# A graph attention kernel: the adjacency turned as packed bytes on VectorE instead of TensorE

## The chip, the core and the metric

The kernel runs on one core of a Trainium2 chip. A core has engines that run side by side, each with its own queue of instructions, taken in order: TensorE (PE in the profile; PEld is its weight load), VectorE (DVE), ScalarE (ACT), GpSimd (POOL), and SyncE (SP), which here only issues DMAs. SBUF is the working memory of 128 partitions, PSUM the memory into which TensorE writes. The metric is the device time of one execution in microseconds; lower is better.

## The reference

Sixty-four graphs of 256 nodes with 512 features go through two layers of attention. `adj` holds one boolean per pair of nodes, and its diagonal may be empty.

```python
def attention(x, mask, heads):                    # both layers, shortened
    q, k, v = heads_of(x @ w_qkv)                 # layer 0: 4 heads of 64; layer 1: 8 heads
    s = einsum('bhid,bhjd->bhij', q, k) * 64 ** -0.5
    s = where(mask[:, None], s, very_negative)
    return (softmax(s) @ v).reshape(...) @ w_out + b_out

h = maximum(layernorm(x), 0);  x = x + attention(h, adj, 4)
h = maximum(layernorm(x), 0);  x = x + attention(layernorm(h) * gamma + beta, adj | eye, 8)
```

A row of layer 0 without any neighbour has equal weights for all keys. Layer 1 always lets a node see itself. All of it is float32.

## The kernel before, in words

**Tiling.** The program takes two graphs at a time (`G = 2`), so there are 32 steps, `s` from 0 to 31. The 512 tokens of a step lie as four blocks of 128 partitions (`NT = 4`). Projections and output products are matrix products by seven block products instead of eight (`PRODUCT`), so each stage is a set of seven groups of matmuls, with sums of blocks made on VectorE and GpSimd (`act_sums0`, `act_sums1`, L404 to L410). Products 4 and 7 of a set share one PSUM bank, as do 2 and 1, and 3 and 5 (`SHARED`): the second of a pair accumulates on top of the first, after the first has been read by `evacuate` (L746) or `accumulate` (L765). Four banks serve these products (`mm_tile`) and four the scores.

**Scores lie transposed:** keys on the partitions, queries along the row. Therefore the mask is needed transposed too. The bytes of `adj` are loaded with query rows on the partitions (`load_adjacency`, L486). Until now `adjacency_cast` (L511) makes them bfloat16 on GpSimd, `adjacency_turn` (L557) turns eight blocks of 128x128 on TensorE into one PSUM bank, and ScalarE copies the bank to `adT` (L568). From `adT`, GpSimd makes the additive masks: `mask0` (L570) for layer 0, which is (value - 1) * 1e30 and then times `ne`, so that a row without neighbours gets zeros; and `mask1` (L579) for layer 1, in which the diagonal is cleared by `offdiag`. `mask_scores` (L988) adds a mask to the scores, `exponentials` (L995) follows on ScalarE. The sums over keys come from `key_halves` (L1000, GpSimd, into `pd`), `turn_keys` (L1007, VectorE's transpose of 32x32 blocks), `key_quarters` (L1013), `turn_sums` (L1064) and `key_sums` (L1074); `normalise` (L1114) multiplies the weighted values by their inverses on GpSimd.

**The order is written out by hand.** `at(period, place, fn, ...)` notes a call with a place in time; at the end all calls are sorted by place and emitted. Each engine takes its instructions in that order. A period is 6.4 places long (6.2 before period 0), and in a full one these stages follow each other on TensorE, each with seven products (`at_set`), the evacuation of product i being placed at its end, at (i + 1) / 7:

- 0.0: the first query and key projection of layer 1 of step s
- 1.0: `combine` of layer 1 of step s - 1, the output product, with the order of products 1, 5, 2, 6, 7, 3, 4
- 2.0 (`AT_X`): a `visit`, which weighs the values of layer 0 of step s + 1 and makes scores of layer 1 of step s; then the value projection `project_v1`, with the order 1, 6, 5, 2, 7, 3, 4
- 3.0: `combine` of layer 0 of step s + 1, whose result is added to `xt`
- 3.5, 4.5, 5.5, 6.2: the second projection of layer 1, a visit, the projections of layer 0 of step s + 2, a visit

So three steps are in work at once. The work on the adjacency of step s + 2 lies in period s: cast at 0.45, turn at 2.5 (in the middle of the value projection), `mask0` at 3.1, `mask1` at 5.85. The bias `bo` of layer 0 is added to `xt` before the output product arrives, by `first_bias` (L506): four instructions on GpSimd, one per block of 128 tokens, at 2.34 and 2.5 for blocks 2 and 3 and at 2.85 and 2.86 for blocks 0 and 1. Steps 0 and 1 have places of their own in a start that is denser (`FIRST_Q0` and its like); there the row `ne` is also turned by TensorE.

Lines that the prediction's steps touch besides: L402 (sums of weights, early in the program), L530 (`neighbours_line`), L606 (`scale_row` on ScalarE), L623 and L600 to L602 (row scales on GpSimd), L675 (`transpose_h` on TensorE), L700 (`turn_blocks`, VectorE's transposes of `h`), L749 to L763 (`evacuate`), L770 to L785 (`accumulate`), L817 and L898 and L914 (matmuls of the projections, the values and the combination), L970 (scores), L1041 (weighing).

Of the kernel before, what the change touches and what calls it, by code (L numbers as in the profile page):

```python
# [8 lines left out]
FP = mybir.dt.float32  # L9
BF = mybir.dt.bfloat16  # L10
U8 = mybir.dt.uint8
I32 = mybir.dt.int32
AF = mybir.ActivationFunctionType
ALU = mybir.AluOpType

EPS = 1e-5
BIG = 1e30
# [298 lines left out]
def fast_path(  # L316
# [19 lines left out]
    nc = tc.nc  # L336
    P = 128
    B, N, D = x.shape
    DH = 64
    G = 2  # L340
    NSTEP = B // G
    NIC = N // P
    NT = G * NIC
# [9 lines left out]
    act = ctx.enter_context(tc.tile_pool(name="act", bufs=1))  # L353
# [10 lines left out]
    def mm_tile(shape, dt=FP, hold=False):  # L364
        tag = next(b for b in banks if b not in held)
        banks.remove(tag)
        banks.append(tag)
        if hold:
            held.add(tag)
        return ps_mm.tile(shape, dt, name="mm", tag=tag)  # L370

    identb = const.tile([P, P], BF, name="identb")
# [17 lines left out]


    NB = 7
    A_OF = {(0, 0): 0, (0, 1): 1, (1, 0): 2, (1, 1): 3}
    B_OF = ((0, 6, 5), (1, 3, 1))
    PRODUCT = {1: (0, 0), 2: (1, 1), 3: (6, 2), 4: (3, 6), 5: (2, 3), 6: (4, 4), 7: (5, 5)}
# [18 lines left out]
    HC, HP0, HP1 = NC // 2, PR0 // 2, PR1 // 2  # L414
    wqk0 = const.tile([P, NB, HC, 2, H0], FP, name="wqk0")
    wv0 = const.tile([P, NB, HC, I0 // 2], FP, name="wv0")
    wo0 = const.tile([P, NB, HP0, HD], FP, name="wo0")
    wqkv1 = const.tile([P, NB, HC, 3, H1], FP, name="wqkv1")
    wo1 = const.tile([P, NB, HP1, HD], FP, name="wo1")
    bo_b = const.tile([P, D], FP, name="bo_b")  # L420
# [42 lines left out]
    def weight_block(wr, n, c):  # L463
# [3 lines left out]
        for i in range(2):  # L467
            blk = A_OF[i, c // HC]
            dst = wqkv1[:, blk, c % HC, n, :] if n < 3 else wo1[:, blk, c % HC, :]
# [4 lines left out]
    S = [dict() for _ in range(NSTEP)]  # L474
# [28 lines left out]
            S[s]["xt"][:, g * NIC:(g + 1) * NIC], x[s * G + g].rearrange("(t p) d -> p t d", p=P)  # L503
        )

    def first_bias(s, t):  # L506
        xt = S[s]["xt"]
        nc.gpsimd.tensor_tensor(xt[:, t, :], xt[:, t, :], bo_b, ALU.add)  # L508


    def adjacency_cast(s):  # L511
        S[s]["adb"] = act.tile([P, NT, N], BF, name="adb", tag="ab")
        nc.gpsimd.tensor_copy(S[s]["adb"], S[s]["ad"])

    def neighbours(s, g):

# [37 lines left out]
        ne = S[s]["ne"] = act.tile([P, T], FP, name="ne")  # L554
        nc.scalar.copy(ne, pn)

    def adjacency_turn(s):  # L557
        adb = S[s]["adb"]
        pa = mm_tile([P, NIC, G, N], BF)
        for g in range(G):  # L560
            for kc in range(NIC):
                for ic in range(NIC):
                    nc.tensor.transpose(  # L563
                        pa[:, kc, g, ic * P:(ic + 1) * P],
                        adb[:, g * NIC + ic, kc * P:(kc + 1) * P], identb,
                    )
        S[s]["adT"] = act.tile([P, NIC, G, N], BF, name="adT", tag="ab")
        nc.scalar.copy(S[s]["adT"], pa)  # L568

    def mask0(s):  # L570

        st = S[s]
        n0 = st["n0"] = act.tile([P, NIC, G, N], BF, name="n0")
        nc.gpsimd.tensor_scalar(n0, st["adT"], -1.0, BIG, op0=ALU.add, op1=ALU.mult)
        for kc in range(NIC):
            v = n0[:, kc].rearrange("p g n -> p (g n)")
            nc.gpsimd.tensor_tensor(v, v, st["ne"], ALU.mult)

    def mask1(s):  # L579
        st = S[s]  # L580
        n1 = st["n1"] = act.tile([P, NIC, G, N], BF, name="n1", bufs=2)
        nc.gpsimd.tensor_scalar(n1, st["adT"], -1.0, BIG, op0=ALU.add, op1=ALU.mult)
        for kc in range(NIC):
            v = n1[:, kc, :, kc * P:(kc + 1) * P]
            nc.gpsimd.tensor_tensor(v, v, offdiag, ALU.mult)
# [82 lines left out]
    def transpose_h(s, lyr, c):  # L668
        st = S[s]
        if c == 0:  # L670
            st["hT"] = act.tile([P, NB, HC, N], FP, name="hT")
        ph = mm_tile([P, G, N])
# [20 lines left out]
    Q, NQ = 32, P // 32  # L693
# [432 lines left out]
    def at(period, place, fn, *args):  # L1126
        events.append((period * (PERIOD if period >= 0 else FIRST) + place, len(events), fn, args))
# [68 lines left out]
    AT_X, AT_C0, AT_QK, AT_Q0, AT_V0, AT_H1, AT_Z = 2.0, 3.0, 3.5, 4.5, 5.5, 6.06, 6.2  # L1196
# [8 lines left out]
    p = NSTEP - 2  # L1205
# [9 lines left out]
    FIRST_C0, FIRST_Q0, FIRST_V0, FIRST_H1 = 3.0, 3.64, 4.64, 5.2  # L1215
# [5 lines left out]
    for s in range(NSTEP):  # L1221

        p = s - 2
        if s == 1:
            p -= 3.93 / FIRST
        at(p - 1 if s != 1 else -2, 3.2 if s == 1 else 5.7 if s < 3 else AT_H1 + 0.01, load_h, s)
        at(p - 1 if s != 1 else -2, 3.2 if s == 1 else 5.7 if s < 3 else 1.0, load_adjacency, s)
        at(p, (2.0, 2.4)[s] if s < 2 else 0.45, adjacency_cast, s)
        for t in range(NT):
            at(p, (0.5 + 0.4 * t, 1.95 + 0.1395 * t)[s] if s < 2 else (0.95, 1.05, 1.2, 1.35)[t], norm0, s, t)  # L1230
            if s == 0:
# [15 lines left out]
        else:  # L1247
            at(p, 2.3 if s == 2 else 0.05, neighbours_line, s)
            at(p, 2.31 if s == 2 else 0.051, neighbours_spread, s)
        at(p, (FIRST_Q0 + 0.1425, 3.583)[s] if s < 2 else 2.5, adjacency_turn, s)  # L1250
        at(p, (FIRST_Q0 + 0.3, 3.74)[s] if s < 2 else 3.1, mask0, s)
        at(p, (FIRST_Q0 + 0.31, 4.43)[s] if s < 2 else 5.85, mask1, s)
        if s == 0:
            at(p, FIRST_C0, first_transposes)
        else:
# [19 lines left out]
        p = s - 1  # L1275
        if s == 0:
            p -= 2.23 / FIRST
        edge = 0 if s == 0 else 1 if s == NSTEP - 1 else 2
# [3 lines left out]
            at(p, AT_X - 0.000145 if s > 1 else 1.2, load_graph, s, 1)  # L1282
            at(p, AT_X + 0.0051 if s > 1 else 1.2, load_graph, s, 0)
        for k, t in enumerate(NORM1):
            at(p, (1.55, 1.5, (2.34, 2.5, 2.85, 2.86)[k])[edge], first_bias, s, t)
        if edge == 2:
            at(p, 2.8, lambda s=s: act_sums0(S[s]["oT0"]))
            at(p, 2.81, lambda s=s: act_sums1(S[s]["oT0"]))
# [26 lines left out]
        p = s  # L1315
        if s < NSTEP - 1:
# [3 lines left out]
            p, place = (s + 1, 1.0) if s < NSTEP - 2 else (s, LAST_QK + 2)  # L1320
# [5 lines left out]
        else:  # L1326
            p = s - 1
# [39 lines left out]
def kernel(tc, *args):  # L1367
    nc = tc.nc
    B, N, _ = args[0].shape
    P = 128  # L1370
    with tc.tile_pool(name="guard", bufs=1) as guard:
        extremes = guard.tile([P, B // 2 * 3 + 4], FP, name="extremes")
        ident = guard.tile([P, P], FP, name="ident")
        make_identity(nc, ident)
        fast_path(tc, *args, ident, extremes)
        safe = guard.tile([1, 1], I32, name="safe")
        with tc.tile_pool(name="gps", bufs=1, space=bass.MemoryType.PSUM) as ps:
            top = guard.tile([P, 1], FP, name="top")
            nc.vector.tensor_reduce(top, extremes, axis=mybir.AxisListType.X, op=ALU.max)
            row = ps.tile([1, P], FP, name="row")  # L1380
            nc.tensor.transpose(row, top, ident)
            all_top = guard.tile([1, 1], FP, name="all_top")
            nc.vector.tensor_reduce(all_top, row, axis=mybir.AxisListType.X, op=ALU.max)
            nc.vector.tensor_scalar(safe, all_top, LIMIT, None, op0=ALU.is_le)
        flag = nc.values_load(safe[0:1, 0:1], min_val=0, max_val=1, skip_runtime_bounds_check_because="a comparison gives 0 or 1")
        with tc.If(flag < 1):
            general_path(tc, *args)
# [29 lines left out]
```

## Time and profile before

| | |
|---|---|
| median of 3 runs | 3113.7 us (3112.78 to 3113.93) |
| profiled execution, its own time | 3115.69 us |
| its span, first to last instruction | 3113.6 us |
| TensorE busy, matmuls | 3091.8 us, 20362 instructions |
| VectorE busy | 2453.8 us, 4371 instructions |
| ScalarE busy | 1235.3 us, 2166 instructions |
| GpSimd busy | 2242.3 us, 2128 instructions |
| L563, TensorE's transposes of the adjacency | 256, 19.5 us busy |
| L568, ScalarE's copy of them | 32, 32.4 us busy |
| L513, GpSimd's cast of the bytes | 32, 33.2 us busy |
| L508, GpSimd's adds of `bo` | 128, of which 124 on `xt`: 156.3 us busy |

How to read it: the span is what the trace covers; the execution's own time has a little around it. Busy time is the union of an engine's instructions. In a timeline, the columns are the start, the duration, the engine, line and operation, what is written from what, shapes, how many neighbouring instructions were merged (x4), and in brackets how long the engine was idle before and what ended that. The granted clock of TensorE was 1.0 throughout.

### The profile page before, as it was taken

The page shows a single profiled execution, that of the slowest core. Times are in us where ns is not written, and L with a number is a line of the kernel's source. Part 1 is how long each engine was busy: PE and PEld are TensorE (multiplying, and loading weights), DVE is VectorE, ACT ScalarE, POOL GpSimd, SP SyncE. Part 2 cuts the span into 40 slices and gives each one's busy share as a digit, 9 for nine tenths or more (in the row PEclk, how much of TensorE's full clock was granted, in tenths as well). Part 3 has the DMA queues.
Part 4 walks back from the last instruction along what each step waited for, and adds up shares of the span by engine and source line. Part 5 has one row for each costly group of instructions (what it writes and reads, how often), then busy time and mean ns, then how long its engine had stood idle before and what let it go on. Part 6 is the DMA issues. An engine that isn't in the chain of part 4 may idle for free.

```text
span 3113.6 us, 55568 instructions
## 1 busy us (share of the span) xinstructions
PE 3091.8 (99%) x20362; PEld 2538.7 (82%) x20362; DVE 2453.8 (79%) x4371; ACT 1235.3 (40%) x2166; POOL 2242.3 (72%) x2128
## 2 busy tenths in 40 slices
PE   8999999999999999999999999999999999999998
PEld 6888888888888888888888888888888888888787
DVE  6877877878877788787788777887777878778766
ACT  4434343344434343443434334443434344343431
POOL 7877776777767767767777677776776776777753
PEclk9999999999999999999999999999999999999999
DMA  4233232332322322223313233222232222331311
GB/s 138 64 98 92 55 91 72 92 93 67 83 71 87 93 87 66 84 72 99 93 53 93 72 91 93 73 79 77 80 93 86 67 82 74 99 93 51 91 34 49
DMA packets 187589, 251.22 MB, mean 81 GB/s; under 512 B 58088, under 2 KB 78192, under 8 KB 187312
## 3 DMA queue, kind: packets, MB, share of 16 engines
q1 hardware_dynamic: 139088, 183.74, 21.0%
q10 hardware_dynamic: 48224, 63.87, 7.0%
q8 instruction: 164, 2.69, 0.4%
q14 instruction: 113, 0.93, 0.1%
HBM read 128.59 MB, written 34.34 MB: 52 GB/s over the span
## 4 chain that ended last, share of the span: by engine, by line
PE 94%; POOL 3%; DMA 1%; DVE 1%; issue 1%; SPq 0%; ACT 0%; ACTq 0%; POOLq 0%; DVEq 0%
PE mm L817 37%; PE mm L914 17%; PE mm L898 11%; PE sc L970 8%; PE mm L864 6%; PE sc L1041 6%; PE mm L1041 5%; PE mm L970 2%; POOL pd L1005 1%; POOL xt L508 1%; PE mm L847 1%; DMA h<-blocks 0%; PE mm L940 0%; DMA out_dram<-xt 0%; PE mm L563 0%
## 5 line engine op out<-in xcount | busy, mean ns | idle before, releaser
L817 PE MATMUL mm<-hT,wqkv 128*128 128x256 f32 x3584 | 788.3, 380 | 0.6 <-DVE qk L757 0.6
L817 PEld LDWEIGHTS mm<-hT,wqkv 128*128 128x128 f32 x3584 | 677.6, 190 | 103.2 <-issue 11.4
L1005 POOL TENSOR_TENSOR pd<-p 128x512 f32<-128x512 f32 x383 | 479.4, 1273 | 337.9 <-ACT p L998 196.2
L914 PE MATMUL mm<-wo,oT 128*128 128x256 f32 x2632 | 586.1, 380 | 4.2 <-DVE xt L774 2.4
L914 PEld LDWEIGHTS mm<-wo,oT 128*128 128x128 f32 x2632 | 497.3, 190 | 83.2 <-issue 9.2
L998 ACT ACTIVATE p<-p 128x512 f32<-128x512 f32 x766 | 440.8, 626 | 118.2 <-DVE p L993 106.2
L993 DVE TENSOR_TENSOR p<-sc,n 128x512 f32<-128x512 f32 x579 | 363.0, 683 | 145.1 <-PE sc L970 145.1
L898 PE MATMUL mm<-wqkv,hT 128*128 128x256 f32 x1792 | 402.1, 382 | 0.4 <-ACT v L751 0.4
L817 PE MATMUL mm<-hT,wqk 128*128 128x256 f32 x1792 | 398.7, 382 | 0.3 <-ACT qk L751 0.2
L817 PEld LDWEIGHTS mm<-hT,wqk 128*128 128x128 f32 x1792 | 338.3, 191 | 55.9 <-issue 10.3
L898 PEld LDWEIGHTS mm<-wqkv,hT 128*128 128x128 f32 x1792 | 335.5, 190 | 54.2 <-issue 10.3
L970 PE MATMUL sc<-qk 64*128 64x256 f32 x2320 | 294.0, 385 | 1.7 <-DVE p L993 1.7
L785 POOL TENSOR_TENSOR xt<-xt,u 128x512 f32<-128x512 f32 x183 | 231.2, 1272 | 78.2 <-DVE xt L774 37.1
L970 PEld LDWEIGHTS sc<-qk 64*128 64x128 f32 x2320 | 218.1, 186 | 62.8 <-issue 27.9
L1011 DVE STREAM_TRANSPOSE turned_p<-pd 128x1024 f32<-128x1024 f32 x192 | 237.1, 1235 | 29.5 <-POOL pd L1005 29.5
L606 ACT ACTIVATE h<-h,mr,r 128x512 f32<-128x512 f32 x252 | 187.6, 803 | 169.6 <-POOL mr L602 169.6
L1116 POOL TENSOR_TENSOR oT<-oT 128x512 f32<-128x512 f32 x188 | 240.0, 1277 | 2.2 <-DMA oT<-line 2.2
L1018 DVE TENSOR_REDUCE part<-turned_p 128x32 f32<-128x1024 f32 x192 | 233.2, 1215 | 4.4
L1041 PE MATMUL sc<-p,v 128*32 128x256 f32 x3152 | 190.8, 382 | 0.0
L864 PE MATMUL mm<-hT,wv 128*128 128x256 f32 x840 | 188.6, 382 | 0.0
L864 PEld LDWEIGHTS mm<-hT,wv 128*128 128x128 f32 x840 | 156.5, 190 | 27.2 <-ACT vT L751 6.2
L1041 PE MATMUL mm<-p,v 128*32 128x256 f32 x2976 | 177.6, 379 | 0.0
(153 smaller groups left out, 4219.2 us busy)
## 6 DMA issues: line engine op xcount, KB each, us to landing
h<-blocks SPq DMA_DIRECT2D x960, 64.0 KB, 2.0
oT<-line SPq DMA_DIRECT2D x376, 128.0 KB, 3.1
h<-in_x_dram SPq DMA_DIRECT2D x31, 1024.0 KB, 8.7
xt<-in_x_dram ACTq DMA_DIRECT2D x60, 512.0 KB, 4.3
out_dram<-xt SPq DMA_DIRECT2D x31, 512.0 KB, 3.1
out_dram<-xt ACTq DMA_DIRECT2D x31, 512.0 KB, 4.5
v<-values ACTq DMA_DIRECT2D x480, 32.0 KB, 1.9
ne<-ne SPq DMA_DIRECT2D x90, 64.0 KB, 2.0
```

The lines of the kernel that those rows point to most:

```text
L817: nc.tensor.matmul(bank[:, k, :], w[:, wa, c, k, a * P:(a + 1) * P], st["hT"][:, ba, c, :], start=first and (k, c) == (0, 0), stop=(k, c) ...
L864: nc.tensor.matmul(bank, wv0[:, wa, c, :], st["hT"][:, ba, c, :], start=first and c == 0, stop=c == HC - 1, skip_group_check=True,)
L898: nc.tensor.matmul(bank[:, t, :], st["hT"][:, ba, c, t * P:(t + 1) * P], wqkv1[:, wa, c, 2, :], start=first and (t, c) == (0, 0), stop=(t, ...
L914: nc.tensor.matmul(bank[:, t, :], oT[:, ba, c, t * P:(t + 1) * P], w[:, wa, c, :], start=first and (t, c) == (0, 0), stop=(t, c) == (NIC - ...
L970: nc.tensor.matmul(sc[g][e][:, kc, :], qk[rows, 1, k0:k0 + P], qk[rows, 0, g * N:(g + 1) * N], start=True, stop=True,)
L993: nc.vector.tensor_tensor(p[e][:, g], sc[e], neg[:, :, g, :], ALU.add)
L998: nc.scalar.activation(p[e][:, g], p[e][:, g], AF.Exp, scale=SCALE)
L1005: nc.gpsimd.tensor_tensor(st["pd"][:, e], p[e][:, :, 0, :], p[e][:, :, 1, :], ALU.add)
L1011: nc.vector.transpose(st["turned_p"], st.pop("pd").rearrange("p e g (b k) -> p (e g b) k", k=32))
L1018: nc.vector.tensor_reduce(st["part", lyr, prs][:, i], st.pop("turned_p"), axis=mybir.AxisListType.X, op=ALU.add)
L1041: nc.tensor.matmul(po[r0:r0 + 32, g, :], (st["v1"][:, g * NIC + kc, pr * P + r0:pr * P + r0 + Q] if lyr else st["v0"][:, r0 // Q, pr, g * ...
L1116: nc.gpsimd.tensor_tensor(dst, dst, invb, ALU.mult)
```

## The change

The bytes are never made bfloat16. Four blocks of 128 query rows lie side by side for the same key, so that one byte from each makes one 32-bit word: GpSimd writes each byte plus 64 (`MARK`) to every fourth place of a tile `both`, which makes each word an ordinary float32 number. VectorE then transposes these words in 32x32 blocks: a call of `adjacency_turn(s, a)` has four instructions, which read partition group `a` and write partition groups 0 to 3; four calls turn everything. The masks read the turned bytes, at every fourth place, and subtract the mark again. TensorE's eight transposes and ScalarE's copy are gone, and with them the use of a PSUM bank.

In full periods three of the calls stand behind the evacuations of the fourth, fifth and sixth product of `combine` of layer 1, and the fourth at the end of that stage behind `turn_blocks`. In steps 0 and 1 the calls stand behind evacuations of the first projections, and `mask0` and `mask1` come later there.

Two of the four pieces of `first_bias` in steps 1 to 30 move from GpSimd (2.34 and 2.5) to VectorE, at 2.6 and 2.61, within the value projection. The other two stay on GpSimd at 2.87 and 2.88.

```diff
-    def first_bias(s, t):
+    def first_bias(s, t, eng=nc.gpsimd):
         xt = S[s]["xt"]
-        nc.gpsimd.tensor_tensor(xt[:, t, :], xt[:, t, :], bo_b, ALU.add)
+        eng.tensor_tensor(xt[:, t, :], xt[:, t, :], bo_b, ALU.add)
-    def adjacency_cast(s):
-        S[s]["adb"] = act.tile([P, NT, N], BF, name="adb", tag="ab")
-        nc.gpsimd.tensor_copy(S[s]["adb"], S[s]["ad"])
+    def adjacency_pack(s):
+        both = S[s]["both"] = act.tile([P, 2, NIC, P, NT], U8, name="both", tag="ab")
+        nc.gpsimd.tensor_scalar(
+            both[:, 0].rearrange("p k j t -> p t k j"), S[s]["ad"].rearrange("p t (k j) -> p t k j", j=P),
+            MARK, None, op0=ALU.add,
+        )
+    def adjacency_turn(s, a):
+        words = S[s]["both"].rearrange("p h k j t -> p (h k j t)").bitcast(FP).rearrange(
+            "p (h k j) -> p h k j", h=2, k=NIC
+        )
+        for b in range(NQ):
+            nc.vector.transpose(
+                words[b * Q:(b + 1) * Q, 1, :, a * Q:(a + 1) * Q], words[a * Q:(a + 1) * Q, 0, :, b * Q:(b + 1) * Q]
+            )
+    def edges(s):
+        return S[s]["both"][:, 1].rearrange("p k i t -> p k t i")
-    def adjacency_turn(s):
...
-                    nc.tensor.transpose(
-                        pa[:, kc, g, ic * P:(ic + 1) * P],
-                        adb[:, g * NIC + ic, kc * P:(kc + 1) * P], identb,
-                    )
-        S[s]["adT"] = act.tile([P, NIC, G, N], BF, name="adT", tag="ab")
-        nc.scalar.copy(S[s]["adT"], pa)
...
-        nc.gpsimd.tensor_scalar(n0, st["adT"], -1.0, BIG, op0=ALU.add, op1=ALU.mult)
+        nc.gpsimd.tensor_scalar(
+            n0.rearrange("p k g (c i) -> p k (g c) i", i=P), edges(s), -1.0 - MARK, BIG, op0=ALU.add, op1=ALU.mult
+        )
...
-        at(p, (FIRST_Q0 + 0.1425, 3.583)[s] if s < 2 else 2.5, adjacency_turn, s)
-        at(p, (FIRST_Q0 + 0.3, 3.74)[s] if s < 2 else 3.1, mask0, s)
-        at(p, (FIRST_Q0 + 0.31, 4.43)[s] if s < 2 else 5.85, mask1, s)
+        for a in range(NQ):
+            at(
+                p, (FIRST_Q0, 3.3)[s] + (a + 3) / 7 - 0.0005 if s < 2 else AT_X - 0.00031 if a > 2 else 1 + (a + 4) / 7 - 0.0005,
+                adjacency_turn, s, a,
+            )
+        at(p, (FIRST_Q0 + 0.87, 4.2)[s] if s < 2 else 3.1, mask0, s)
+        at(p, (FIRST_Q0 + 0.88, 4.43)[s] if s < 2 else 5.85, mask1, s)
...
-            at(p, (1.55, 1.5, (2.34, 2.5, 2.85, 2.86)[k])[edge], first_bias, s, t)
+            if edge < 2 or k > 1:
+                at(p, (1.55, 1.5, 2.85 + 0.01 * k)[edge], first_bias, s, t)
+            else:
+                at(p, 2.6 + 0.01 * k, first_bias, s, t, nc.vector)
```

`mask1` changes in the same way as `mask0`.

More of the change, by code (lines that the diff above doesn't have):

```diff
@@ L392, in fast_path @@
     NB = 7
+    MARK = 64.0
     A_OF = {(0, 0): 0, (0, 1): 1, (1, 0): 2, (1, 1): 3}
@@ L555, in neighbours_turn @@
         nc.scalar.copy(ne, pn)
-    def adjacency_turn(s):
[L558 to L563, printed above, removed]
-                        pa[:, kc, g, ic * P:(ic + 1) * P],
-                        adb[:, g * NIC + ic, kc * P:(kc + 1) * P], identb,
-                    )
-        S[s]["adT"] = act.tile([P, NIC, G, N], BF, name="adT", tag="ab")
-        nc.scalar.copy(S[s]["adT"], pa)
     def mask0(s):
@@ L581, in mask1 @@
         n1 = st["n1"] = act.tile([P, NIC, G, N], BF, name="n1", bufs=2)
-        nc.gpsimd.tensor_scalar(n1, st["adT"], -1.0, BIG, op0=ALU.add, op1=ALU.mult)
+        nc.gpsimd.tensor_scalar(
+            n1.rearrange("p k g (c i) -> p k (g c) i", i=P), edges(s), -1.0 - MARK, BIG, op0=ALU.add, op1=ALU.mult
+        )
         for kc in range(NIC):
@@ L1227, in fast_path @@
         at(p - 1 if s != 1 else -2, 3.2 if s == 1 else 5.7 if s < 3 else 1.0, load_adjacency, s)
-        at(p, (2.0, 2.4)[s] if s < 2 else 0.45, adjacency_cast, s)
+        at(p, (2.0, 2.4)[s] if s < 2 else 0.45, adjacency_pack, s)
         for t in range(NT):
@@ L1249, in fast_path @@
             at(p, 2.31 if s == 2 else 0.051, neighbours_spread, s)
-        at(p, (FIRST_Q0 + 0.1425, 3.583)[s] if s < 2 else 2.5, adjacency_turn, s)
-        at(p, (FIRST_Q0 + 0.3, 3.74)[s] if s < 2 else 3.1, mask0, s)
-        at(p, (FIRST_Q0 + 0.31, 4.43)[s] if s < 2 else 5.85, mask1, s)
+        for a in range(NQ):
+            at(
+                p, (FIRST_Q0, 3.3)[s] + (a + 3) / 7 - 0.0005 if s < 2 else AT_X - 0.00031 if a > 2 else 1 + (a + 4) / 7 - 0.0005,
+                adjacency_turn, s, a,
+            )
+        at(p, (FIRST_Q0 + 0.87, 4.2)[s] if s < 2 else 3.1, mask0, s)
+        at(p, (FIRST_Q0 + 0.88, 4.43)[s] if s < 2 else 5.85, mask1, s)
         if s == 0:
```

## Prediction

> **What bounds it now.** I read busy shares and chain first, then PE's timeline of one step, then VectorE's and GpSimd's beside it. The page:
>
> ```profile
> PE 3091.8 (99%) x20362; PEld 2538.7 (82%) x20362; DVE 2453.8 (79%) x4371; ACT 1235.3 (40%) x2166; POOL 2242.3 (72%) x2128
> PE 94%; POOL 3%; DMA 1%; DVE 1%; issue 1%; SPq 0%; ACT 0%; ACTq 0%; POOLq 0%; DVEq 0%
> ```
>
> TensorE ends the program: 94% of the chain is its own work. The chain in order of time gives the length of a step (first projection of one period to that of the next), and PE's timeline in that step shows the transposes:
>
> ```profile
> 1515.08 12.28 PE mm L817 x56
> 1610.75 12.28 PE mm L817 x56
> ...
> 1546.62 7.17 PE L898 MATMUL mm<-wqkv,hT 128*128 128x256 f32 x32
> 1553.63 0.61 PE L563 MATMUL mm<-identb,adb 128*128 128x128 bf16 x8
> 1554.08 5.40 PE L898 MATMUL mm<-wqkv,hT 128*128 128x256 f32 x24
> ```
>
> A step is 95.67 us and most are exactly that: PE is full, so microseconds taken from or added to its queue count one for one.
>
> **Step 1, transposes leave PE.** The durations of single matmuls overlap (0.22 each), so I take starts: 1554.08 - 1553.63 = 0.45 us per step. Thirty steps: -13.6 us. The first two sets, at 15.8 and 48.2, gain nothing: PE then waits for an evacuation anyway (0.23 for ACT's copy at 16.67, 0.20 for VectorE's L753 at 49.17). The Trainium skill ("VectorE: DVE Perf Modes", The three transpose paths) prices a bf16 128x128 transpose at 390 ns on TensorE and 311 ns on VectorE. By it eight would cost PE 3.1 us and the estimated gain would be 94 us; the trace has 0.45 us for eight in a row, and it decides. ACT loses its 1.01 us copy (L568); at 40% busy that is worth nothing.
>
> **Step 2, 16 transposes of 32 partitions x 64 words enter VectorE.** L1071 has this size: 0.96 us for four in a row, so 3.84 us per step. VectorE in the old place and the new one:
>
> ```profile
> 1534.30 0.69 DVE L772 TENSOR_TENSOR u<-mm,u 128x512 f32<-128x512 f32 x1
> 1536.03 0.69 DVE L774 TENSOR_TENSOR xt<-mm,xt 128x512 f32<-128x512 f32 x1 [1.04 <-PE mm L914]
> 1537.76 0.69 DVE L781 TENSOR_TENSOR xt<-mm,xt 128x512 f32<-128x512 f32 x1 [1.03 <-PE mm L914]
> 1539.48 0.69 DVE L779 TENSOR_TENSOR xt<-mm,xt 128x512 f32<-128x512 f32 x1 [1.03 <-PE mm L914]
> 1540.09 2.48 DVE L700 STREAM_TRANSPOSE blocks<-h 128x512 f32<-128x512 f32 x4
> 1544.13 2.48 DVE L993 TENSOR_TENSOR p<-sc,n 128x512 f32<-128x512 f32 x4 [1.56 <-PE sc L970]
> ...
> 1553.46 0.68 DVE L755 TENSOR_TENSOR v<-mm,v 128x512 f32<-128x512 f32 x1
> 1556.06 0.69 DVE L757 TENSOR_TENSOR v<-mm,v 128x512 f32<-128x512 f32 x1 [1.92 <-PE mm L898]
> ```
>
> The four groups fall into the idle 1.04, 1.03, 1.03 and 1.56: hidden by PE's combine and weighing. Bounds: 0.20 us each (32x32, L1071) to 0.31 (L530, 32x128, 1.23 for four). At 0.31 the first three end 0.2, 0.4 and 0.6 late; behind them wait the evacuations L774, L781, L779, whose banks PE wants again a whole product (1.73) later, and 0.3 of lateness is left at L993, at most 0.3 us of PE. I take 0.24 and nothing. No gain is possible.
>
> **Step 3, the two adds of xt and bo_b on VectorE.** They queue between L755 (ends 1554.14) and L757, into the last gap above. Alone such an add takes 0.69 (L408 on VectorE at the end of the program), two 1.3: they would fit. But both inputs lie in SBUF, while GpSimd is running:
>
> ```profile
> 12.63 1.27 POOL L405 TENSOR_TENSOR hT<-hT 128x512 f32<-128x512 f32 x1 [0.83 <-DVE hT L742]
> 13.98 1.59 POOL L408 TENSOR_TENSOR hT<-hT 128x512 f32<-128x512 f32 x1
> 15.54 1.71 POOL L409 TENSOR_TENSOR hT<-hT 128x512 f32<-128x512 f32 x1
> ...
> 13.00 1.45 DVE L402 TENSOR_TENSOR wqk<-wqk 128x512 f32<-128x512 f32 x1
> 14.48 1.64 DVE L402 TENSOR_TENSOR wqk<-wqk 128x512 f32<-128x512 f32 x1
> ...
> 1566.18 2.49 POOL L785 TENSOR_TENSOR xt<-xt,u 128x512 f32<-128x512 f32 x2
> 1567.50 1.24 DVE L1083 CUSTOM_DVE_ANT_0 keys<-keys 32x64 f32<-32x64 f32 x1
> ```
>
> VectorE's two-input add ends 0.55 after GpSimd's running instruction (13.90 to 14.45; 15.57 to 16.12), and GpSimd's next is stretched to end 1.12 after VectorE's (14.45 to 15.57). Small L1083 takes 0.21 with GpSimd idle, and 1.24 here, until GpSimd ends at 1568.67. So such an instruction waits for GpSimd's current one. GpSimd where the adds will run:
>
> ```profile
> 1552.44 2.49 POOL L1005 TENSOR_TENSOR pd<-p 128x512 f32<-128x512 f32 x2 [0.63 <-DVE turned_p L1011]
> 1554.89 1.26 POOL L508 TENSOR_TENSOR xt<-xt,bo_b 128x512 f32<-128x512 f32 x1
> 1556.12 1.27 POOL L1116 TENSOR_TENSOR oT<-oT 128x512 f32<-128x512 f32 x1
> ```
>
> L508 goes, so L1116 moves up to 1554.9. Both engines start from the end of L1011, so the phase is fixed. First add: issued 1554.1, waits for L1005's end at 1554.93, ends 1555.48. L1116 ends at 1555.48 + 1.12 = 1556.60. Second add ends 1557.15, L757 at 1557.75 (back to back these come 0.6 apart). Behind L757 stands PE: it evacuates product 7 of the value projection, and product 4 accumulates in the same bank. Product 4 starts at 1557.58 now and would start at 1557.13 with the transposes gone. A PE start after such an evacuation comes 0.14 later (L774 ends 224.32, L914 starts 224.46): 1557.89. Stall 0.76 us per step, 22.8 in thirty. Bounds: no wait, stall 0; and one add losing its turn once more, as the L1083 at 801.85 did (1.36 us, though GpSimd's instruction ended at 801.90): 1.27 more, 2.03. I take 0.76, since L402 is the same add against the same kind of GpSimd instruction. The data isn't in question: L508 began the first piece at 1550.53.
>
> **Step 4, GpSimd.** It loses two adds of 1.27; L1116's 0.34 of stretch is given back, so the remaining two adds and mask0 come some 0.7 earlier. Combine's L776 now waits for L508 (5.6 us, ten times), which reaches PE as 2.4 us (L914 after L774, five times): -2.4. The packing and both masks now touch every fourth byte, which no row shows. Low end: the dense rows, 1.04 (L513, L574), since no GpSimd row goes under 1.0 ns per element. High end: L1005's 2.49 ns per element, 2.55 us. I take 1.05, the nearest row by operation. The cover is this step's slack: the packing precedes the second L1116 (ends 1525.54, PE's combine starts 1527.20), mask1 precedes L408 (ends 1513.81, PE wants it for product 6 at 1516.76) and L1005, which VectorE's L1011 waits for. It bears some 0.8 us more on each instruction; at 2.55 the packing and the lateness passed on by mask1 put L1116 at 1527.9, which is 0.7 us of PE per step, 21 in all. The skill ("GPSIMD Engine Reference", Performance pitfalls for Q7 kernels) puts a 50% surcharge on read steps over 8 bytes; the step is 4, so by it an estimated 0. No run here shows it.
>
> **Step 5, the start.** In step 0 mask0 and mask1 (19.0 to 25.3, GpSimd otherwise idle) now follow the last transposes of VectorE (about 28.9), so run from 29.3 to 35.0, ahead of the row scales of step 1 (L623 to L602, 28.28 to 30.14) and of the pd sums. Row scales end near 36.9; ACT's four L606 (33.63 to 37.92) end near 40.8, and PE's L675 (38.31) starts its last block 2.4 later. Bounds 0 (absorbed by VectorE's later idle, such as 3.67 before 57.77) and 4. I take +2.4.
>
> **Sum.** -13.6 + 22.8 - 2.4 + 2.4 = +9.2. The profiled execution has a span of 3113.6 and took 3115.7: 3124.9 in its terms. It lies 2.0 above the median 3113.7, so against the median: **3123**.
>
> **Rivals.**
> - *The adds fit* (faster). If they aren't held as L402 was, or only one is, L757 is done by 1556.98 and there is no stall: 3113.7 - 13.6 - 2.4 + 2.4 = 3100. It decides at both adds done by 1556.4, 1.13 each. For: the uncontended 0.69 and a gap that fits. Against: L402, L1083, and a GpSimd without a pause from 1552.44. 0.27.
> - *Partly held* (no change). If GpSimd's L1116 runs elsewhere so that one wait shrinks, the stall is about the 0.45 won: 3113. 0.08.
> - *Byte steps are dear.* Step 4's high end on top of mine, 3130 to 3144. For: three instructions of unknown price. Against: slack. 0.10.
> - *The transposes aren't gone from the path*: VectorE the bound in place of PE. 76.6 of 95.6 us are busy in this step; with 3.8 and 3.3 that is 84 of 96. Too little: under 0.01, counted with the forecast.
>
> Forecast 0.55, 3117 to 3130. About 0.2% (6.2 us) is what a measurement can tell. Slower: forecast and byte rival less the forecast's low edge (0.10), 0.55. Faster: first rival and a little of the second, 0.28. Same: 0.17. Both signs hold much, so the range spans 3098 (first rival, start at its low end) to 3133.
>
> **What would show it.** Right: L563 gone; the new adds near 1.4 and 1.65 us instead of 0.69, ending 0.55 after a GpSimd instruction; PE's L898 with a gap of 0.7 before product 4, waiting on VectorE's L757; a step of 95.98. Wrong: adds of 0.69, a step of 95.22; or GpSimd's packing and masks well over 1.1 us; or gaps of PE before the scores, from the transposes.

## The result, and the profile after

The changed kernel takes 3156.93 us (median of 4 runs, 3156.44 to 3157.76); the kernel before, on the same chip, 3113.53. The ratio is 1.014, with a 95% interval of [1.0122, 1.0158]: slower, and 24 us above the upper end of the range. Times and ratios of the experiments below are given in the same way, always against the kernel before. The profiled execution has a span of 3154.8, so 41.2 more than before.

Busy shares and chain of the page after the change:

```profile
PE 3096.0 (98%) x20106; PEld 2523.6 (80%) x20106; DVE 2660.8 (84%) x4943; ACT 1205.1 (38%) x2134; POOL 2259.9 (72%) x2068
PE 68%; DVE 8%; DMA 7%; POOL 5%; ACT 5%; issue 3%; ACTq 3%; SPq 1%; DVEq 0%; POOLq 0%
```

TensorE's 256 transposes are gone from the count, but its share of the chain (the work that ended last, followed back step by step to what released it) has fallen from 94% to 68%. The end of the program now hangs on other engines in a third of its length, on DMAs and ScalarE's DMA queue (ACTq) among them. Where they come in, the view of waits says (total, times, longest; of TensorE's rows those that are new or longer than before):

```profile
PE mm L905 <- DVE v L764: 19.0, 30, 1.8
PE mm L921 <- ACT u L777: 12.1, 28, 1.2
PE sc L977 <- DVE p L1000: 6.2, 2, 5.3
PE mm L824 <- ACT wqkv L472: 4.2, 1, 4.2
```

(Lines have moved by one at `first_bias` and by seven from `transpose_h` on.) The first row is the value projection behind the two new adds, the second the combination of layer 1, which had no such wait, the last two are the start. The groups by shape (count, busy us and mean ns, idle before) price what is new:

```profile
L524 DVE STREAM_TRANSPOSE both<-both 32x64 f32<-32x64 f32 x512 | 120.5, 235 | 8.2
L514 POOL TENSOR_SCALAR both<-ad 128x1024 uint8<-128x1024 uint8 x32 | 98.4, 3075 | 0.0
L509 DVE TENSOR_TENSOR xt<-xt,bo_b 128x512 f32<-128x512 f32 x60 | 92.1, 1572 | 0.0
L587 POOL TENSOR_SCALAR n<-both 128x1024 bf16<-128x1024 uint8 x32 | 33.4, 1044 | 2.2
```

Transposes (235 ns, 3.77 us per step) and masks (1.04) cost what was assumed; the packing, 3.08 us, is above its upper bound.

**Where the 41.2 us are.** From the starts of TensorE's stages: the first value projection starts at 121.68 instead of 109.40, so the start costs 12.3. From there to the start of the last value projection it is 28.9 longer, about 1.0 in most steps (96.7 instead of 95.67). Within a step two stages grow: the value projection takes 13.03 instead of 12.69, and the combination of layer 1 mostly 12.76 to 12.95 instead of 12.18. One shrinks: the combination of layer 0 no longer waits for late adds in some steps, 4.3 us less in all. All other stages in this stretch take 1994.0 us in sum instead of 1994.7, so the granted clock (0.998 instead of 1.0) is not the cause. The time after the start of the last value projection is the same 38.9.

*The value projection.* Its timeline:

```profile
1484.44 2.50 POOL L1012 TENSOR_TENSOR pd<-p 128x512 f32<-128x512 f32 x2 [1.81 <-DVE turned_p L1018]
1486.06 3.10 DVE L509 TENSOR_TENSOR xt<-xt,bo_b 128x512 f32<-128x512 f32 x2
1486.90 1.72 POOL L1123 TENSOR_TENSOR oT<-oT 128x512 f32<-128x512 f32 x1
...
1489.09 0.68 DVE L764 TENSOR_TENSOR v<-mm,v 128x512 f32<-128x512 f32 x1
...
1489.82 2.00 PE L905 MATMUL mm<-wqkv,hT 128*128 128x256 f32 x8 [0.57 <-DVE v L764]
```

The two adds take 3.10 together, GpSimd's L1123 between them is stretched to 1.72, VectorE's L764 comes behind both, and TensorE waits for it.

*The combination of layer 1.* First after the change:

```profile
1550.30 8.17 ACTq L895 DMA_DIRECT2D v<-values  x10
1551.28 3.08 POOL L514 TENSOR_SCALAR both<-ad 128x1024 uint8<-128x1024 uint8 x1
...
1554.39 0.39 SPq L489 DMA_DIRECT2D ad<-in_adj_dram  x1
...
1558.51 0.58 ACT L777 COPY u<-mm 128x512 f32<-128x512 f32 x1 [7.65 <-DMA v<-values]
...
1559.15 8.90 PE L921 MATMUL mm<-wo,oT 128*128 128x256 f32 x40 [0.29 <-ACT u L777]
```

and then the same place before:

```profile
1522.30 6.29 ACTq L888 DMA_DIRECT2D v<-values  x10
...
1524.33 0.39 SPq L488 DMA_DIRECT2D ad<-in_adj_dram  x1
...
1529.12 0.59 ACT L770 COPY u<-mm 128x512 f32<-128x512 f32 x1 [6.27 <-DMA v<-values]
```

ScalarE issues ten DMAs of `move_values` and only then copies the first product of the combination to `u`; the second product of that PSUM bank cannot start on TensorE before the copy has read the first. The group of DMAs takes 8.17 instead of 6.29. A narrower window of the timeline after the change shows where:

```profile
1553.42 1.24 ACTq L895 DMA_DIRECT2D v<-values  x2
1554.39 0.39 SPq L489 DMA_DIRECT2D ad<-in_adj_dram  x1
...
1556.67 1.80 ACTq L895 DMA_DIRECT2D v<-values  x3
```

Single DMAs start 0.64 apart; the seventh starts at 1554.07, the eighth only at 1556.67, 1.96 us late. By the trace's semaphore records it waits on a DMA semaphore (eight are used in turn) on which the load of the next bytes signals; that load, on SyncE's queue, landed at 1556.65. The load in turn was issued at 1554.39, 0.03 after GpSimd had finished packing: there is one tile `ad`, and packing reads it. In the kernel before, the load landed at 1526.67 and the DMA started at 1526.70, 0.64 after its predecessor: in time, with nothing to spare. It is the same in each of the 28 full steps of the changed kernel: the load is issued 0.03 after the packing ends, and the eighth DMA starts 0.02 after the load's landing, 1.8 to 3.6 after its predecessor. So the chain is packing, load of the next bytes, ScalarE's eighth DMA, its copy to `u`, TensorE.

*The start*, after the change:

```profile
114.36 3.94 DVE L524 STREAM_TRANSPOSE both<-both 32x64 f32<-32x64 f32 x16
118.33 2.48 DVE L1000 TENSOR_TENSOR p<-sc,n 128x512 f32<-128x512 f32 x4
119.08 2.67 PE L977 MATMUL sc<-qk 64*128 64x256 f32 x8 [5.27 <-DVE p L1000]
```

Period 0 has no combination of layer 1 (there is no step before it), so the evacuations between which the transposes of step 2 should stand do not exist. All sixteen come in one piece of 3.94 us ahead of the masking of scores, and TensorE waits 5.27 us. Earlier, GpSimd's masks and the packing stand ahead of row scales and sums:

```profile
37.56 3.09 POOL L514 TENSOR_SCALAR both<-ad 128x1024 uint8<-128x1024 uint8 x1
...
40.58 2.52 POOL L1012 TENSOR_TENSOR pd<-p 128x512 f32<-128x512 f32 x2
...
43.13 1.25 DVE L1018 STREAM_TRANSPOSE turned_p<-pd 128x1024 f32<-128x1024 f32 x1 [8.64 <-POOL pd L1012]
...
54.11 2.26 PE L824 MATMUL mm<-hT,wqk 128*128 128x256 f32 x7 [4.24 <-ACT wqkv L472]
```

The first `turned_p` came 7.3 earlier in the kernel before:

```profile
35.83 1.25 DVE L1011 STREAM_TRANSPOSE turned_p<-pd 128x1024 f32<-128x1024 f32 x1 [2.31 <-POOL pd L1005]
```

### The profile page after: what moved, and what is told of

Its sections match the earlier page's. It is cut to its first block, busy times and chain, and to the rows that moved or that the text cites. A ratio compares the mean times of both kernels' runs of the same rounds, so it can differ in the third digit from the quotient of the medians.

```text
span 3154.8 us, 55501 instructions
## 1 busy us (share of the span) xinstructions
PE 3096.0 (98%) x20106; PEld 2523.6 (80%) x20106; DVE 2660.8 (84%) x4943; ACT 1205.1 (38%) x2134; POOL 2259.9 (72%) x2068
## 4 chain that ended last, share of the span: by engine, by line
PE 68%; DVE 8%; DMA 7%; POOL 5%; ACT 5%; issue 3%; ACTq 3%; SPq 1%; DVEq 0%; POOLq 0%
PE mm L824 26%; PE mm L921 14%; PE sc L977 6%; PE mm L871 6%; PE sc L1048 5%; PE mm L1048 5%; PE mm L905 4%; ACT p L1005 3%; ACTq L895 3%; POOL both L514 3%; DMA h<-blocks 2%; DMA ad<-in_adj_dram 2%; DVE xt L509 2%; POOL pd L1012 1%; PE mm L977 1%
## 5 line engine op out<-in xcount | busy, mean ns | idle before, releaser
L921 PE MATMUL mm<-wo,oT 128*128 128x256 f32 x2632 | 594.2, 382 | 12.6 <-ACT u L777 12.1
L792 POOL TENSOR_TENSOR xt<-xt,u 128x512 f32<-128x512 f32 x183 | 231.4, 1271 | 92.5 <-DVE xt L781 41.2
L1123 POOL TENSOR_TENSOR oT<-oT 128x512 f32<-128x512 f32 x188 | 252.7, 1344 | 3.9 <-DMA oT<-line 3.9
L777 ACT COPY u<-mm 128x512 f32<-128x512 f32 x62 | 36.3, 585 | 435.0 <-PE mm L921 221.8
```

The costliest lines, as they stand in the source:

```text
L921: nc.tensor.matmul(bank[:, t, :], oT[:, ba, c, t * P:(t + 1) * P], w[:, wa, c, :], start=first and (t, c) == (0, 0), stop=(t, c) == (NIC - ...
L1123: nc.gpsimd.tensor_tensor(dst, dst, invb, ALU.mult)
```

## The experiments

**Theory** after the comparison: three causes. The adds wait for GpSimd (about 0.8 us per step); the packing delays a load and with it ScalarE's DMA (about 0.65 per step); the transposes and GpSimd's work lengthen the start. The rival for the second cause is that GpSimd as such is late with its sums; for the third, that only the packing's price counts there.

**bias_back**: the adds back to GpSimd, all else as changed.

```
-            if edge < 2 or k > 1: ...
-            else: at(p, 2.6 + 0.01 * k, first_bias, s, t, nc.vector)
+            at(p, (1.55, 1.5, (2.34, 2.5, 2.85, 2.86)[k])[edge], first_bias, s, t)
```

> The changed kernel with all four pieces of first_bias on GpSimd again, at their old places; the transposes stay on VectorE. Theory: the two adds on VectorE wait for GpSimd's running instruction, hold up L764's evacuation of product 7 and cost PE 0.78 us in each of 30 value projections (13.03 us now); without them that stage is 12.25 us, the combination of layer 1 stays at about 12.8, so 3157 - 23 = 3134 us, perhaps 2 more because the late adds of GpSimd hold up the combination of layer 0 again. Rival (the transposes fill VectorE, the adds are innocent): the stage stays at 13.0 and the time near 3157.

Measured 3139.03, 1.008 [1.0064, 1.0097]. The value projection takes 12.19, the combination of layer 1 still about 12.9, a step mostly 95.8 to 96.1, with further waits for GpSimd's late adds (TensorE behind VectorE's L781, 5.5 us in 13 places), and the first value projection starts at 123.00; so the time is 5 us over the forecast. The adds are one cause, worth 18 us here.

**before_bias**: the reverse, the two adds of the change put into the kernel before, with TensorE's transposes kept.

> The kernel before with one part of the change alone: two of the four adds on VectorE at 2.6 and 2.61. Theory: the adds wait for GpSimd as in the changed kernel, product 4 starts 0.3 us late in each step (the transposes of the adjacency still stand between, so there is 0.45 us more room than in the changed kernel): value projection 13.02 in place of 12.70, 30 times, less 2.4 us of late adds on GpSimd: 3120 to 3124. Rival (the adds fit if VectorE has no transposes): 3111.

Measured 3121.98, 1.0025 [1.0015, 1.0035]. Value projection 13.02, steps 96.00 instead of 95.67. The group of adds:

```profile
L508 DVE TENSOR_TENSOR xt<-xt,bo_b 128x512 f32<-128x512 f32 x60 | 92.0, 1571 | 0.0
```

This is the price in the changed kernel too (13.03 and 1572 ns), with no transposes on VectorE and no packing. Step 3 stands alone and is right.

**pack_act**: the packing on ScalarE; nothing else is changed from the kernel after.

```
-        nc.gpsimd.tensor_scalar(..., MARK, None, op0=ALU.add)
+        nc.scalar.activation(..., AF.Copy, bias=MARK)
```

> The changed kernel with the packing of the bytes on ScalarE (a copy plus 64) instead of GpSimd, same place; the two adds stay on VectorE. Theory (the byte writes at every fourth place are dear on GpSimd, not in general): about 1.0 us on ScalarE, which is idle 60% of the time; the combination of layer 1 falls to 12.2 us (-19), the value projection stays at 13.03, and the start loses some of its 12 us: 3130 to 3136. Rival (single-byte writes at a distance of four are dear for any engine): about 3 us on ScalarE as well, its copies of products come late and the time stays above 3145.

Measured 3137.02, 1.0074 [1.0057, 1.009]. Steps 96.0, combination of layer 1 back at 12.18; the start has won nothing (first value projection at 122.56). Its timeline at the place in question:

```profile
1541.68 1.37 ACT L514 ACTIVATE both<-ad 128x1024 uint8<-128x1024 uint8 x1 [2.92 <-DMA v<-values]
1542.45 0.51 ACTq L895 DMA_DIRECT2D v<-values  x1
1543.01 5.74 ACTq L895 DMA_DIRECT2D v<-values  x9
1543.07 0.39 SPq L489 DMA_DIRECT2D ad<-in_adj_dram  x1
```

The packing takes 1.37 us and is done 0.6 after the group's first DMA; the load is issued right then and lands at 1545.34, 1.5 before the eighth DMA's turn (1546.86), and the ten DMAs follow without a gap.

**pool_busy**: pack_act, with a GpSimd instruction of the same length put back that nobody waits for. It writes bytes of `bo_b`, in place of those of `ad`, to the half of `both` that is overwritten later. This tells the two theories of the combination apart: GpSimd is as late as in the kernel after, but the load is not.

> The kernel with the packing on ScalarE and two adds on VectorE (3137.0), and in addition GpSimd does, where the packing stood, one byte scatter of the same size, of bytes of bo_b into the half of the tile that the transposes will overwrite, so that it is as busy as in the changed kernel, but nothing waits for it to load the next bytes. Theory (the load of the next bytes, held by the long packing, holds a DMA of ScalarE and so its copy u): the combination of layer 1 stays at 12.18 us, the time at 3137 plus up to 4 from the start. Rival (GpSimd's products and sums come too late behind 3 us): the combination at 12.8, 3155 or more.

Measured 3148.08, 1.0107 [1.0091, 1.0122]:

```profile
1551.93 5.74 ACTq L900 DMA_DIRECT2D v<-values  x9
1551.99 0.39 SPq L489 DMA_DIRECT2D ad<-in_adj_dram  x1
1552.45 3.07 POOL L518 TENSOR_SCALAR both<-bo_b 128x1024 uint8<-128x1024 uint8 x1
1556.35 12.29 PE L926 MATMUL mm<-wo,oT 128*128 128x256 f32 x56
```

With 3.07 us on GpSimd in the same place the combination takes 12.23 and a step 96.05. The lateness of GpSimd costs 0.05 of the 0.65; the rest is the load, which here lands before the eighth DMA's turn in every full step. The whole is 11 us longer than pack_act all the same, 7 over the forecast: 7.5 of them are the start (first value projection at 130.0 instead of 122.6; the instruction waits 5.8 us for the load of `bo_b` once), and 2.9 lie in the steps.

**ad_later**: the load of the next bytes placed later in the program (2.3 instead of 1.0), so that ScalarE's DMA would not stand behind it.

> The changed kernel with the load of the next step's adjacency bytes at place 2.3 instead of 1.0; nothing else. Theory: the packing takes 3.07 us in place of 1.04, the next load of the bytes waits for it (same tile), and one of ScalarE's DMAs of the values waits for that load to land, since both use the same one of eight DMA semaphores; ScalarE's copy u is behind that DMA and PE waits for it 0.6 to 0.7 us in each combination of layer 1. With the load elsewhere in the order that wait goes: stage 12.2 instead of 12.8, about -19 us, 3138. Rival (the long packing delays GpSimd's own products and sums, which the combination needs): no change, 3157 within 3.

Measured 3158.81, 1.0142 [1.0126, 1.0159]: nothing gained. It did not do what it was meant to: the load was still issued right behind the packing (packing ends at 1557.23, load issued at 1557.26, landed at 1559.51, ScalarE's eighth DMA at 1559.53). The load also kept its semaphore. So the run decides nothing between theory and rival, and shows the same 0.02 once more. Whether two tiles `ad` in turn would take the wait away was not tried.

**pack_act_bias_back**: both edits together, so that only the transposes on VectorE, with the packing on ScalarE, and the later masks of the start remain of the change.

> Both: packing on ScalarE, all four adds on GpSimd, transposes on VectorE. Theory: the two costs are separate, so both go: a step of 95.22 us in place of 96.7 (13.6 us gained over the kernel before in thirty steps), the start still some 6 to 10 us longer than before: 3106 to 3113. Rival (VectorE's transposes themselves hold up PE): over 3120.

Measured 3116.23, 1.0009 [1.0, 1.0019]. Steps of 95.18 in the first two thirds, which is 0.49 under the kernel before; combination of layer 1 12.18, so VectorE's transposes do not hold up TensorE there. In the last third of the steps late adds take part of the gain back; from the first value projection to the last it is 11.5. All of that is lost at the start: the first value projection begins at 120.45, 11 late. The time is 3 us over the forecast.

**step2_pe**: from there, step 2 alone cast by GpSimd and turned by TensorE as before.

> The kernel with packing on ScalarE and all adds on GpSimd (3116.2), with step 2 alone turned by TensorE; steps 0 and 1 by VectorE. Theory: of the 12 us lost before the first value projection, 4 to 5 are the sixteen transposes of step 2, which in period 0 stand together in front of a mask addition that PE waits for; so the projection begins near 116 in place of 120.5, the time is 3111 to 3113. Rival (all of it is from steps 0 and 1): no change.

Measured 3112.27, 0.9992 [0.9983, 1.0002]; first value projection at 113.95. So between the two profiled executions step 2 in the new way costs 6.5 us of start; 4.0 of that is TensorE's wait for the masking of scores, behind the sixteen transposes (5.7 us in the run above, 1.7 here). Between the medians the whole is 4.0, as this kernel's runs spread over 5 us (3108.43 to 3113.70).

**hybrid**: steps 0 to 2 in the old way, with the old places of their masks; from step 3 packing on ScalarE, transposes on VectorE, all adds on GpSimd.

> Steps 0 to 2 as in the kernel before (bytes to bfloat16, TensorE's transposes, masks at their old places); from step 3 on the packing on ScalarE, VectorE's transposes and all four adds on GpSimd. Theory: the start's loss (the first value projection begins at 120.5 us in place of 109.4) comes from the transposes of step 2 in front of a mask addition, since no combination stands there in period 0, and from the masks and the packing of steps 0 and 1 that now precede other work of GpSimd; so here that time is as before, 109 to 110, and the steps are 95.2 instead of 95.67: 3113.5 - 13.6 + at most 3 for late adds = 3100 to 3103. Rival (the start pays later whatever is done): above 3108.

Measured 3105.62, 0.9975 [0.9966, 0.9984]: faster than both. First value projection at 108.49, most steps 95.18. The forecast for this run was 2.6 us too low, because the first six steps still take 96.5 to 97.5, where GpSimd comes late with its adds (TensorE behind VectorE's L800, 4.6 us in ten places) and its sums (behind L409, 3.5 in five).

**hybrid_one_add**: hybrid, with the add of block 2 on VectorE at 2.6.

> As the kernel with steps 0 to 2 turned by TensorE, but one of the four adds (block 2) on VectorE at 2.6. Theory: an add on VectorE waits for GpSimd's running instruction, but one alone (about 1.4 us) ends some 0.3 us before the evacuation of product 7 must begin, so the value projection stays at 12.2; and GpSimd, rid of one add, no longer holds up the combination of layer 0 (4.7 us in all, PE waiting for VectorE's L781): 3095 to 3100, 2 to 5 us under its sibling. Rival (any wait on GpSimd there is paid by PE): value projection over 12.5, 3108 or more.

Measured 3112.30, 0.9997 [0.9988, 1.0006]: 12 us over the forecast, and 7 over hybrid. The value projection takes 12.19, so one add does fit, at 1.42 us. But the following combination of layer 0 takes 6.77 instead of 6.3. GpSimd's timeline, and TensorE's row of the waits:

```profile
1456.94 2.50 POOL L1031 TENSOR_TENSOR pd<-p 128x512 f32<-128x512 f32 x2 [1.79 <-DVE turned_p L1037]
1459.39 1.72 POOL L509 TENSOR_TENSOR xt<-xt,bo_b 128x512 f32<-128x512 f32 x1
1461.08 1.27 POOL L1142 TENSOR_TENSOR oT<-oT 128x512 f32<-128x512 f32 x1
```

```profile
PE mm L940 <- DVE xt L800: 14.9, 29, 0.7
```

The add that was taken off GpSimd had stood in a pause (now 1.79 us of idle time) and cost GpSimd nothing; the one left behind is stretched to 1.72. So all that follows on GpSimd is later, and with it the later adds that L800 waits for.

**second_add**: the other choice. Block 2's add stays in the pause on GpSimd, block 3's goes to VectorE.

```
+            if edge == 2 and k == 1:
+                at(p, 2.6, first_bias, s, t, nc.vector)
```

> Steps 0 to 2 turned by TensorE, packing on ScalarE, and one add on VectorE as in the kernel with one add, but the other one: block 3, whose add on GpSimd stands after the second pd pair, where GpSimd has no pause; the add of block 2 stays in GpSimd's pause of 1.8 us. Theory: the add on VectorE still waits (about 1.4 us) and still ends in time for product 7, GpSimd's following work comes 0.9 us earlier instead of 0.45 later, and the combination of layer 0 is back at 6.3 us: steps of 95.2, without the 4 to 8 us of late adds that the kernel without any add on VectorE pays: 3097 to 3102. Rival (any add on VectorE there costs): 3106 or more.

Measured **3101.55, 0.9957 [0.9944, 0.9971]**, within the forecast and the best of all. Its timeline and chain:

```profile
1454.50 2.50 POOL L1031 TENSOR_TENSOR pd<-p 128x512 f32<-128x512 f32 x2
...
1456.06 1.48 DVE L509 TENSOR_TENSOR xt<-xt,bo_b 128x512 f32<-128x512 f32 x1
...
1456.95 1.73 POOL L1142 TENSOR_TENSOR oT<-oT 128x512 f32<-128x512 f32 x1
```

```profile
PE 92%; POOL 3%; DVE 2%; DMA 2%; issue 1%; ACT 0%; SPq 0%; ACTq 0%; DVEq 0%; POOLq 0%
```

GpSimd has no pause before L1031, L509 on VectorE ends 0.55 after it, and what follows on GpSimd is 0.8 earlier than with the add (1.27 off, 0.46 of stretch on). Value projection 12.19, combinations 6.29 and 12.18, steps 95.17. TensorE is at 92% of the chain again.

**adds_early**: hybrid with both adds on VectorE at 2.287, inside GpSimd's pause, to see whether it is GpSimd that makes them slow.

> The kernel with steps 0 to 2 turned by TensorE and packing on ScalarE, and both adds on VectorE, but at 2.287, right after the evacuation of product 6, where GpSimd has nothing to do until VectorE's turn_keys ends. Theory (the adds are slow for GpSimd's sake only): they take 0.69 us each instead of 1.57, and the value projection, 13.02 with the adds at 2.6, is 12.2 to 12.5 here; 3098 to 3108. Rival (such an add is slow on VectorE by itself, or the load of xt holds it): over 1 us each, value projection at 13 or more, 3125.

```profile
L509 DVE TENSOR_TENSOR xt<-xt,bo_b 128x512 f32<-128x512 f32 x60 | 41.8, 736 | 5.6 <-DMA h<-blocks 3.1 <-DMA xt<-in_x_dram 2.4
```

736 ns instead of 1572, with the same shapes and tiles. The mean hides two kinds: 46 of the 60 adds met no GpSimd instruction and took 0.68 to 0.69 us; the other 14 began beside one, and all but two of them ended 0.55 after it. In the changed kernel and in before_bias every one of the 60 adds ended 0.55 after the GpSimd instruction beside which it began. So the slowness is GpSimd's running instruction. The time is 3113.34, 0.9997 [0.9988, 1.0007]: at that place the adds push the evacuations before product 4 (value projection 12.34 to 14, TensorE behind L781 8.8 us in eleven places) and wait for the load of `xt`. The mechanism was right, the gain wasn't there.

**pack_dense** and **dense_bytes** ask why the packing costs 3.08. pack_dense walks the blocks innermost, so that GpSimd writes its bytes one behind the other and reads 256 bytes apart:

```
-            both[:, 0].rearrange("p k j t -> p t k j"), S[s]["ad"].rearrange("p t (k j) -> p t k j", j=P),
+            both[:, 0], S[s]["ad"].rearrange("p t (k j) -> p k j t", j=P),
```

> The changed kernel, packing on GpSimd, but walking so that the bytes are written one after the other and read at steps of 256 bytes. Theory (the scattered writing of single bytes makes the 3.07 us, reading at a distance is cheap, as the masks show with 1.04): 1.0 to 1.6 us, the combination of layer 1 at 12.2 us, 3132 to 3138. Rival (reads at 256 bytes are as dear): 3 us or more and 3157 or more.

It got slower: 3176.32, 1.0198 [1.0183, 1.0214], combination of layer 1 about 13.4; TensorE now waits there for GpSimd's sums too (L406, 12.8 us). Either the read step of 256 is dear or the byte output itself, so dense_bytes is pool_busy with the extra instruction dense on both sides.

> The kernel of pool_busy, whose extra GpSimd instruction (64 added to 1024 bytes per partition, nobody needs the result) now reads and writes its bytes one behind the other instead of at every fourth place. Theory: what costs is the step of the writing, and a dense instruction goes at about 1.0 ns per element like the cast of the kernel before (1.04 us) and the masks (1.04): 1.05 us. Rival: GpSimd is slow at any byte output, whatever the step: 2.9 to 3.1 us, as the 3.09 of pool_busy. Between the two, some 2 us: each has a part. The steps stay at 96.0 to 96.1 us as in pool_busy, since the instruction is in nobody's way in either case; the whole goes by the start as before, 3140 to 3148 us.

One run: 3145.74, beside 3115.01 for the kernel before. The rows of pack_dense and of dense_bytes:

```profile
L514 POOL TENSOR_SCALAR both<-ad 128x1024 uint8<-128x1024 uint8 x32 | 119.0, 3719 | 0.0
```

```profile
L518 POOL TENSOR_SCALAR both<-bo_b 128x1024 uint8<-128x1024 uint8 x32 | 89.1, 2785 | 6.0 <-DMA bo_b<-in_L_gnn_bo_dram 6.0
```

Dense bytes in, dense bytes out: 2.79. To every fourth byte, 3.07 to 3.09. The masks, which read every fourth byte and write bfloat16, take 1.04, and so did the old cast. So it is the byte output that is dear on GpSimd, by a factor of 2.7, and the step of the writing adds only a tenth. (The 32 packings of the changed kernel all take 3.06 to 3.09, whatever runs beside them.) The theory of scattered writes falls. Why byte output is dear, and whether a plain copy of bytes would be, stays open.

## Why the prediction was wrong, step by step

The direction was right, the size was not: +9.2 forecast, +41.2 in the span, +43.4 in the medians.

- **Step 1 (-13.6): right.** Where nothing else changes, a step is 95.17 to 95.18, which is 0.49 less; 0.45 had been read off the starts (30 times 0.45 is 13.5).
- **Step 2 (0, transposes hidden): right in full steps, wrong in period 0.** They take 235 ns, four in 0.97 to 0.99, and combination and weighing hide them (12.18 and 3.59 in pack_act, hybrid and second_add). But the places had been checked in one steady step only; in the first one the cover does not exist, and step 2's sixteen in one piece cost 4.0 (medians) to 6.5 us (profiled executions; step2_pe).
- **Step 3 (+22.8): right**, the best part of it. The two adds take 1.43 and 1.75 us against 1.4 and 1.65 forecast, each ending 0.55 after a GpSimd instruction as forecast, and the value projection takes 13.03 instead of 12.19 without them, or 0.84 per step against 0.76; before_bias shows it by itself and adds_early shows that GpSimd is the reason. The rivals in which the adds fit are out; that one add fits is shown by hybrid_one_add and second_add.
- **Step 4 (-2.4) is the step that failed**, twice. Its price: for the packing 1.05 was taken and 2.55 was the upper bound, both from rows that write bfloat16 or float32; no row of the kernel before writes more than one byte per partition, and 3.08 was measured. The masks' 1.05 was right (1.04), and so was the end of L776's waits (2.4 us of TensorE, and no such row after). Its path: lateness of GpSimd's sums was priced, but pool_busy shows that as 0.05 us per step. What counts is that the packing holds the tile `ad`, and so the next load, and so a DMA of another queue that shares a semaphore with that load: some 0.6 per step, 19 us in all. The high-end estimate of 0.7 per step, and with it the rival of dear byte steps, came near this by luck: it named the right instruction, but reached TensorE through GpSimd's lateness. The row that could have warned was there in the profile before: ScalarE's copy to `u` waited 6.27 us on DMAs of `move_values`, so the copy already stood behind a DMA queue, and the load was issued in the midst of these DMAs.
- **Step 5 (+2.4, bounds 0 and 4): too small.** The start costs 12.3. Some 4.0 to 6.5 of it is step 2's transposes, which this step did not count. The masks of step 0 ran about where it had put them (28.5 to 34.4, against 29.3 to 35.0). What it left out is the packing behind them, 3.09 us instead of the cast's 1.04 ahead of the first sums over keys; masks and packing together make `turned_p` 7.3 late. How the rest divides between the masks and the packing, no run here shows; in hybrid, where steps 0 to 2 go the old way, the whole loss is gone (first value projection at 108.49).

Put in order, with the forecast in brackets, by the sums of the stages: transposes gone -14.2 (-13.6), adds +27.3 (+22.8), late adds gone -4.3 (-2.4), combination of layer 1 +20.7 (0), start +12.3 (+2.4). Of the 20.7, pool_busy gives 1.7 to GpSimd's lateness, and 19.0 are left to the load. The other stages are 0.7 shorter in sum, which makes the 41.2 but for rounding.

The Trainium skill ("GPSIMD Engine Reference", Performance pitfalls for Q7 kernels), with its 50% for read steps over 8 bytes, was cited as being without effect at a step of 4; the masks' 1.04 agrees. pack_dense has a step of 256 and takes 3.72 where dense_bytes takes 2.79, so here the surcharge is a third and not a half.

## What to carry to other kernels

A layout that saves work on the bound engine has to be priced by the type it writes, not only by its operation and its element count; where the trace has no row that writes the type, the bound on that price is open at the top. For an instruction that reads a loaded tile with one buffer, follow also the next load of that tile, and whatever waits for that load on any queue. And a place "between" other instructions should be looked up in the first period as well as in a steady one.

## What the runs showed of the hardware

- A 128x512 float32 add on VectorE with both inputs in SBUF takes 0.68 to 0.69 us where GpSimd pauses (adds_early); beside running GpSimd instructions it ends 0.55 after the one it met, 1.57 on average (before_bias). The GpSimd instruction that follows is stretched from 1.27 to 1.72. Moving an add to VectorE gives GpSimd back 0.8 us of 1.27 where GpSimd has no pause (second_add).
- GpSimd: 128x1024 bytes to bfloat16 1.04 us, bytes to bytes 2.79 dense, 3.08 with a write step of 4, 3.72 with a read step of 256. ScalarE packs the same bytes with the write step of 4 in 1.37.
- A DMA of one queue started 0.02 us after the landing of a load on another queue that shares its semaphore, in each of 28 full steps, and stood still for 1.96 us until then in the step shown, although their data have nothing to do with each other.
- Eight bfloat16 transposes of 128x128 in a row are worth 0.45 to 0.49 us on TensorE, as the steps of hybrid and second_add show.
